# The end of the last batch in a two-layer graph kernel: a new order for GpSimd's work, for the norms of two older batches and for the last four rows

## The chip, the cores and the metric

The kernel runs on one NeuronCore of one Trainium2 chip. The metric is the device time of one execution in microseconds; 2596.31 us is the median of three runs of the kernel before (2594.66 to 2597.35). Five engines work from queues of their own: TensorE (PE in the profile, its weight loads PEld), VectorE (DVE), ScalarE (ACT), GpSimd (POOL) and SyncE (SP), which here issues nearly all the DMAs. An engine takes its instructions in the order in which the program lists them for that engine, and waits on semaphores of the others.

## The reference

32 batches of 512 rows by 512 features pass through two layers that share one 512x512 adjacency matrix of zeros and ones:

```
q, k, v = x@Wq+bq, x@Wk+bk, x@Wv+bv           # 8 heads of 64
s = softmax(q@k.T / 8, masked where adj == 0)
x = layernorm(x + s@v)                        # layer 0
x = layernorm(x + (adj@x)@weight + bias)      # layer 1
```

The layer norms go along the features, without gain or offset.

## The kernel before

**Tiling.** A batch is four blocks of 128 rows (`NB`) and four blocks of 128 features (`DB`). A 128x512 float32 result fills one PSUM bank; there are eight, all from one pool (`bank`, line 200). `X[b]` holds the rows of batch b in SBUF. The residuals, the norms and the output all happen in place in it.

**Products in halves.** Operands are split into a rounded high half and a rest, so that three passes of fast matmuls give float32 accuracy. For the second layer, `aggregate` (line 510) multiplies by the adjacency and yields, for each block d of features, one bank. `split_y` (line 504) turns that bank into three factors: the high one on ScalarE (line 303), the rest on VectorE (line 306), and their difference "both" on GpSimd or VectorE (line 309). `convolve` (line 555) then multiplies the factors by the weight: for each block r of rows, four matmuls each of HIGH and REST into a "near" bank and four of BOTH into a "far" bank. `add_row` (line 564) adds near (line 547) and far (line 551) to `X[b]` on VectorE. `add_bias` (line 530) adds the bias to a row block on GpSimd. `survey` lists `statistics` (lines 467 and 468, VectorE); `norm` lists a square root on ScalarE (line 471), its inverse with four shifts on VectorE (lines 476 and 478), and four `normalise` on ScalarE (line 483). `store` issues the output DMA from SP.

**The order of the work** is written out by hand: the pools run under a manual schedule, and the Python order of the calls is the order of each engine's queue. `run` executes a list of units, and `merge` lays other units behind them one by one. `iteration(b)` overlaps the attention of batch b, the projections of b+1 and the second layer of b-1. The first 31 batches go through it, and the change doesn't touch it, except that the norms and the store of the batch numbered 29 are left to what follows.

**The end**, which the change is about, consists of `last_halves(31)` and of the program's last part (line 928 on). Batches are numbered 0 to 31, so three of them are open here: 29 (rows 2 and 3 of its second layer, its second norm, its store), 30 (its whole second layer) and 31 (half of its attention and all that follows).

- `last_halves` ends the attention of 31. In between, it runs the last two row blocks of `convolve(29)`, adds their rows and biases, splits `X[30]` by feature blocks (`split`, line 486: the high on ScalarE, line 493, and the low on VectorE, line 494), folds the sums of the exponentials (`folds`, lines 645 and 647), sends them through memory and back to another layout (`pass_parts` and `fetch_parts`, lines 654 and 661), aggregates batch 30 (line 516), and then norms and stores batch 29 and adds the last attention results to `X[31]` (`add_up`, lines 667 to 669, and `last_residual`, lines 695 and 697).
- The program's last part takes statistics of `X[31]`, convolves batch 30, and then for each row block c: normalises `X[31]`'s block, adds batch 30's row c, splits `X[31]`'s block into a high (ScalarE, line 527) and a low (GpSimd, line 528), adds batch 30's bias (GpSimd, line 531) and takes its statistics. Then come the four biases of 31, `aggregate_rows(31)` (line 539: for each row block, four banks with one low and one high matmul each), its `split_y`, `convolve(31)` (48 matmuls), batch 30's norm and store, and row by row batch 31's near and far sums, statistics, root, inverse, normalise and store. `judge` (lines 701 to 706) and one small matmul (line 964) form a verdict (line 965) on whether the fast path's numbers can be trusted. A slower general kernel stands behind a branch on it and isn't executed here.

Of the kernel before, what the change touches and what calls it, by code (L numbers as in the profile page):

```python
# [182 lines left out]
def fast_kernel(ctx: ExitStack, tc, verdict, x, adj, Wq, bq, Wk, bk, Wv, bv, W1, b1, out):  # L183
    nc = tc.nc
    B, N, D = x.shape
    H = Wq.shape[1] // HD
    HP = H // 2
    NB = N // P
    DB = D // P
# [10 lines left out]
    def bank(*shape):  # L200

        return psum.tile([P, *shape], FP, name="bank", tag="bank", bufs=8)

    def plain(t):

        return t.bitcast(FP)
# [95 lines left out]
    def split_high(high, a):  # L302
        nc.scalar.activation(high, a, AF.Copy, scale=EPSILON * SHRINK)

    def split_rest(rest, high, a):
        nc.vector.scalar_tensor_tensor(rest, plain(high), -1.0 / EPSILON, a, op0=ALU.mult, op1=ALU.add)  # L306
# [18 lines left out]
    def factors():  # L325
        return [work.tile([P, DB, N], FR, name=f"factors{f}", bufs=1) for f in (HIGH, REST, BOTH)]
# [143 lines left out]
    def square_root(t, slots):  # L470
        nc.scalar.activation(RSTD[t][:, slots], STAT[t][:, slots, 1], AF.Sqrt, bias=eps)

    def invert_root(t, slots):

        rstd = RSTD[t][:, slots]
        nc.vector.reciprocal(rstd, rstd)
        for slot in range(slots.start, slots.stop):
            nc.vector.tensor_scalar(SHIFT[t][:, slot:slot + 1], STAT[t][:, slot, 0:1], RSTD[t][:, slot:slot + 1], -1.0,  # L478
                                    op0=ALU.mult, op1=ALU.mult)
# [6 lines left out]
    def split(b, d):  # L486

        cols = X[b][:, :, d * P:(d + 1) * P]
        room = d // PAIRS if b == B - 2 else 0
        high = work.tile([P, NB, P], FR, name="high", tag=f"q{room}", bufs=PAIRS)  # L490
        low = work.tile([P, NB, P], FR, name="low", tag=f"k{room}", bufs=PAIRS)
        HIGHS[b, d], LOWS[b, d] = high, low
        nc.scalar.activation(high, cols, AF.Copy)  # L493
        (nc.vector if b == B - 2 else nc.gpsimd).tensor_sub(low, cols, plain(high))  # L494

    def store(b, blocks=None):
        for c in blocks or ():
            nc.sync.dma_start(out[b, c * P:(c + 1) * P, :], X[b][:, c, :])
        if blocks is None:
            nc.sync.dma_start(out[b].rearrange("(c p) d -> p c d", p=P), X[b])  # L500

    YT = {}

    def split_y(b, d, pm, engine=nc.gpsimd):
        high, rest, both = (YT[b][f][:, d, :] for f in range(3))
        split_high(high, pm)
        split_rest(rest, high, pm)
        split_both(both, high, rest, engine)
# [24 lines left out]
    def aggregate_rows(b):  # L533

        banks = [bank(N) for _ in range(DB)]
        for c in range(NB):
            for d, pm in enumerate(banks):
                for part in (LOWS[b, c], HIGHS[b, c]):
                    nc.tensor.matmul(pm, part[:, d * P:(d + 1) * P], adjT[:, c, :],
                                     start=(c == 0 and part is LOWS[b, c]), stop=(c == NB - 1 and part is HIGHS[b, c]))  # L540
        YT[b] = factors()
        for d, pm in enumerate(banks):
            split_y(b, d, pm, nc.gpsimd if d < 2 else nc.vector)

    def add_near(b, r, near):
        row = X[b][:, r, :]
# [2 lines left out]
    def add_far(b, r, far):  # L549
        row = X[b][:, r, :]  # L550
        nc.vector.tensor_add(row, far, row)  # L551

    NEAR, FAR = {}, {}

    def convolve(b, passes):

        yt = YT[b]
        for r, f, blocks in passes:
            if (b, r) not in NEAR:
                NEAR[b, r], FAR[b, r] = bank(N), bank(N)  # L560
            one_pass(f, (FAR if f == BOTH else NEAR)[b, r], lambda f, d: yt[f][:, d, r * P:(r + 1) * P],
                     lambda f, d: w1[:, f, d, :], blocks)

    def add_row(b, r):
        add_near(b, r, NEAR.pop((b, r)))
        add_far(b, r, FAR.pop((b, r)))

    def whole(r):
        return [(r, f, range(DB)) for f in (HIGH, REST, BOTH)]
# [129 lines left out]
    def judge():  # L699
        seen = consts.tile([P, 3], FP, name="seen")  # L700
        nc.vector.tensor_reduce(seen[:, 0:2], watched.rearrange("p k c h -> p k (c h)"), axis=AX.X, op=ALU.add)
        nc.vector.tensor_reduce(seen[:, 2:3], inexact, axis=AX.X, op=ALU.add)
        well = consts.tile([P, 4], FP, name="well")
        nc.vector.tensor_scalar(well[:, 0:2], seen[:, 0:2], BOUND, None, op0=ALU.is_le)
        nc.vector.tensor_scalar(well[:, 2:3], seen[:, 2:3], 0.0, None, op0=ALU.is_equal)
        nc.vector.tensor_reduce(well[:, 3:4], well[:, 0:3], axis=AX.X, op=ALU.min)
        return well[:, 3:4]

    def run(units):
        for unit in units:  # L710
            unit[0](*unit[1:])
# [42 lines left out]
    def norm(t, which):  # L754

        if t - which < 0:
            return []
        lo, hi = which * NB, (which + 1) * NB
        return [(square_root, t, slice(lo, hi)), (invert_root, t, slice(lo, hi))] + [
            (normalise, t, slot) for slot in range(lo, hi)]  # L760
# [4 lines left out]
    def survey(b, which=1):  # L765

        return [(statistics, b, which, c) for c in range(NB)] if b >= 0 else []
# [5 lines left out]
    def biases(b):  # L773
        return [(add_bias, b, c) for c in range(NB)] if b >= 0 else []

    def merge(units, behind):

        merged = []
        for k in range(max(len(units), len(behind))):
            merged += units[k:k + 1] + (behind[k] if k < len(behind) else [])  # L780
        return merged
# [78 lines left out]
    def last_halves(b):  # L860

        splits, gathered = aggregation(b - 1)
        young = norm(b - 1, 0)
        attend(b, 0)
        turn_out(b, 0)
        attend(b, 1)
        turn_out(b, 1)
        fetch_parts(b, 0)
        add_up(b, 0)
        take_scores(b, 1)  # L870
        turn_back(b, 0)
        turn_back(b, 1)
        run(young[:1] + [(last_residual, b, 0), (last_residual, b, 1)] + young[1:2] + folds(b, 1)[:1])
        for r in range(NB // 2, NB):
            convolve(b - 2, whole(r))
        run([(add_row, b - 2, r) for r in range(NB // 2, NB)] + biases(b - 2)[NB // 2:] + young[2:] + splits)
        attend(b, 2)
        turn_out(b, 2)
        attend(b, 3)
        turn_out(b, 3)  # L880
        turn_back(b, 2)
        turn_back(b, 3)
        run(folds(b, 1)[1:] + [(pass_parts, b, 1), (fetch_parts, b, 1)])
        run(merge(gathered, [[unit] for unit in survey(b - 2)[NB // 2:]]) + norm(b - 1, 1))
        store(b - 2)
        run([(add_up, b, 1), (last_residual, b, 2), (last_residual, b, 3)])

    units = projections(0)
    ends = project_first_two()
# [36 lines left out]
    last_halves(B - 1)  # L926

    t = B - 1
    ahead, seen, next_ = norm(t, 0), survey(t - 1), norm(t, 1)
    run(survey(t, 0) + ahead[:2])  # L930
    convolve(t - 1, FIRST_TWO + whole(2) + whole(3))
    for c in range(NB):
        run(ahead[2 + c:3 + c] + [(add_row, t - 1, c)])
        split_rows(t, c)
        run(biases(t - 1)[c:c + 1] + seen[c:c + 1])
    run(biases(t))
    aggregate_rows(t)
    convolve(t, FIRST_TWO)
    run([(add_near, t, r, NEAR.pop((t, r))) for r in range(2)])
    run(next_)  # L940
    store(t - 1)
    well = judge()
    for table, name, shape in ((STAT, "stat", (2 * NB, 2)), (RSTD, "rstd", (2 * NB,)), (SHIFT, "shift", (2 * NB,))):
        table[t + 1] = work.tile([P, *shape], FP, name=name, bufs=3)
    for r in range(NB):
        if r < 2:
            add_far(t, r, FAR.pop((t, r)))
        else:
            convolve(t, whole(r))
            add_row(t, r)  # L950
        statistics(t, 1, r)
        slot = slice(NB + r, NB + r + 1)
        square_root(t + 1, slot)
        invert_root(t + 1, slot)
        if r == NB - 1:
            row = X[t][:, r, :]
            nc.vector.tensor_scalar(row, row, STAT[t + 1][:, NB + r, 0:1], RSTD[t + 1][:, NB + r:NB + r + 1],
                                    op0=ALU.subtract, op1=ALU.mult)
        else:
            normalise(t + 1, NB + r)  # L960
        store(t, [r])
        if r == 1:
            pm = bank(N)
            nc.tensor.matmul(pm[0:1, 0:1], well, ones[:, 0:1], start=True, stop=True)
            nc.vector.tensor_scalar(verdict, pm[0:1, 0:1], P - 0.5, None, op0=ALU.is_lt)


# [22 lines left out]
```

## Time and profile before

| | us |
|---|---|
| median of three runs | 2596.31 |
| the profiled execution, its own time | 2597.58 |
| its span in the trace | 2595.2 |
| TensorE busy | 2570.6 (99%) |
| VectorE busy | 2071.4 (80%) |
| ScalarE busy | 1527.2 (59%) |
| GpSimd busy | 1747.4 (67%) |
| last matmul of `convolve(30)` ends | about 2550.95 |
| first matmul of `aggregate_rows(31)` | 2552.46 |
| first matmul of `convolve(31)` | 2564.42 |
| last matmul ends | about 2584.3 |
| last VectorE instruction (line 957) ends | about 2590.5 |

Times are in microseconds from the start of the span. A line of the timeline gives the start, the duration (of the whole group, where equal instructions are merged), the engine, the line of the source, the operation with output and input, the number of instructions, and in brackets the idle time of that engine just before and what released it. In a table of windows, each engine has its busy time in the stretch and, in brackets, its number of instructions; PEclk is the TensorE clock granted, with 1.00 for full speed.

### The profile page before, as it was taken

To read this page: it belongs to the slowest core of one execution; us is meant where nothing else is said; L and a number is where in the kernel's file an instruction comes from. 1 tells how busy PE (TensorE), PEld (TensorE's weight loads), DVE (VectorE), ACT (ScalarE), POOL (GpSimd) and SP (SyncE) were. 2 spreads that over 40 slices of the span, in tenths; PEclk is the share of its full clock that TensorE was granted. 3 is DMA by queue.
4 is the path that set the end of the run, shared out by engine and by line. 5 is a ranking of instruction groups with operands and counts; after the bars stand their busy time and mean duration, and the time that the engine had idled before them with its cause. 6 is when DMAs were issued, how large, how long until landed. Compare 5 with 4: busy or idle time off the path is not lost.

```text
span 2595.2 us, 35714 instructions
## 1 busy us (share of the span) xinstructions
PE 2570.6 (99%) x11326; PEld 1696.3 (65%) x11326; DVE 2071.4 (80%) x3801; ACT 1527.2 (59%) x2539; POOL 1747.4 (67%) x1099
## 2 busy tenths in 40 slices
PE   9999999999999999999999999999999999999997
PEld 6666666766666666767666666667666666766665
DVE  8878888788787788877877878878778878788776
ACT  5566655656555666556565566655566655656553
POOL 4776676666676666767666766667666676666674
PEclk9999999999999999999999999999999999999998
DMA  8555554554545645446545455454464454554511
GB/s 256 164 165 140 161 148 120 171 144 157 166 100 161 176 130 158 130 134 172 141 159 148 112 164 162 145 161 117 144 176 137 154 142 124 167 146 155 165 41 51
DMA packets 674898, 380.47 MB, mean 147 GB/s; under 512 B 586896, under 2 KB 590992, under 8 KB 674704
## 3 DMA queue, kind: packets, MB, share of 16 engines
q1 hardware_dynamic: 674416, 377.61, 51.2%
q8 instruction: 92, 1.51, 0.2%
q14 instruction: 102, 0.84, 0.1%
q10 hardware_dynamic: 288, 0.52, 0.1%
HBM read 303.57 MB, written 74.45 MB: 146 GB/s over the span
## 4 chain that ended last, share of the span: by engine, by line
PE 96%; DVE 1%; SPq 1%; POOL 1%; ACT 0%; DMA 0%; issue 0%; DVEq 0%; POOLq 0%; ACTq 0%
PE bank L408 52%; PE bank L592 17%; PE bank L615 17%; PE bank L516 9%; SPq L232 0%; DVE bnst L467 0%; POOL xlast L531 0%; POOL xs L531 0%; SPq L635 0%; DMA stream<-kept_k 0%; SPq L240 0%; DMA xin<-in_x_dram 0%; DVE wv L314 0%; SPq L661 0%; POOL factors L309 0%
## 5 line engine op out<-in xcount | busy, mean ns | idle before, releaser
L596 ACT ACTIVATE e<-e 128x1024 f32<-128x1024 f32 x512 | 526.0, 1055 | 308.1 <-DVE e L594 269.2
L408 PE MATMUL bank<-factors,stream 128*128 128x512 f32 x3012 | 704.3, 393 | 1.0 <-ACT stream L313 0.7
L408 PEld LDWEIGHTS bank<-factors,stream 128*128 128x128 f32 x3012 | 560.2, 188 | 165.7 <-DVE e L594 23.5
L607 POOL TENSOR_TENSOR es<-es,e 128x1024 f32<-128x1024 f32 x256 | 616.0, 2406 | 20.1
L594 DVE SCALAR_TENSOR_TENSOR e<-gap,bank 128x512 f32<-128x512 uint8 x1024 | 617.6, 677 | 12.2 <-PE bank L592 12.2
L607 POOL TENSOR_TENSOR es<-e 128x1024 f32<-128x1024 f32 x128 | 305.9, 2390 | 426.4 <-ACT e L596 426.4
L592 PE MATMUL bank<-q,k 64*128 64x512 f32 x2048 | 465.0, 599 | 0.7 <-DVE e L594 0.7
L615 PE MATMUL bank<-e,v 128*64 128x512 f32 x2048 | 453.6, 595 | 0.0
L592 PEld LDWEIGHTS bank<-q,k 64*128 64x128 f32 x2048 | 204.2, 186 | 260.0 <-issue 158.0
L408 PE MATMUL bank<-w,factors 128*128 128x512 f32 x1536 | 358.3, 392 | 3.7 <-POOL factors L309 1.9
L408 PE MATMUL bank<-wv,factors 128*128 128x512 f32 x1536 | 353.5, 389 | 0.0
L309 POOL TENSOR_TENSOR factors<-factors,factors 128x512 fp32r<-128x512 f32 x253 | 322.6, 1295 | 34.4 <-DVE factors L306 30.3
L681 ACT ACTIVATE rows<-rows,zero,inverse 128x64 f32<-128x64 f32 x992 | 335.1, 430 | 6.9 <-DVE inverse L668 6.9
L408 PEld LDWEIGHTS bank<-w,factors 128*128 128x128 f32 x1536 | 289.4, 189 | 66.3 <-DVE factors L306 3.1
L408 PEld LDWEIGHTS bank<-wv,factors 128*128 128x128 f32 x1536 | 288.2, 188 | 60.6 <-DVE e L594 0.8
L615 PEld LDWEIGHTS bank<-e,v 128*64 128x64 f32 x2048 | 141.4, 137 | 278.4 <-issue 263.9
L493 ACT ACTIVATE high<-xs 128x512 fp32r<-128x512 f32 x124 | 74.4, 627 | 333.3 <-PE bank L516 333.2
L494 POOL TENSOR_TENSOR low<-xs,high 128x512 fp32r<-128x512 f32 x120 | 154.2, 1297 | 156.1 <-PE bank L516 156.1
L531 POOL TENSOR_TENSOR xs<-xs,b_r 128x512 f32<-128x512 f32 x124 | 160.2, 1292 | 129.1 <-DVE xs L551 129.1
L627 DVE STREAM_TRANSPOSE attT<-bank 128x512 f32<-128x512 f32 x124 | 87.5, 707 | 156.3 <-PE bank L615 156.3
L483 ACT ACTIVATE xs<-xs,shift,rstd 128x512 f32<-128x512 f32 x248 | 181.6, 805 | 27.3 <-DVE shift L478 27.3
L685 POOL TENSOR_TENSOR xs<-xs,rows 128x512 f32<-128x512 f32 x124 | 160.6, 1306 | 22.6 <-ACT rows L681 14.2
(98 smaller groups left out, 2449.3 us busy)
## 6 DMA issues: line engine op xcount, KB each, us to landing
stream<-kept_q SPq DMA_DIRECT2D x124, 768.0 KB, 5.7
stream<-kept_k SPq DMA_DIRECT2D x124, 768.0 KB, 4.4
xin<-in_x_dram SPq DMA_DIRECT2D x496, 64.0 KB, 2.3
turned<-attT SPq DMA_DIRECT2D x124, 256.0 KB, 3.0
rows<-turned SPq DMA_DIRECT2D x496, 64.0 KB, 2.5
xs<-in_x_dram SPq DMA_DIRECT2D x31, 1024.0 KB, 6.4
out_dram<-xs SPq DMA_DIRECT2D x31, 1024.0 KB, 5.2
part<-passed SPq DMA_DIRECT2D x256, 8.0 KB, 1.7
```

What stands on the lines that cost most here:

```text
L309: engine.tensor_sub(both, plain(high), plain(rest))
L408: nc.tensor.matmul(pm, left(f, d), right(f, d), start=(f != REST and d == 0), stop=(f != HIGH and d == DB - 1))
L483: nc.scalar.activation(row, row, AF.Identity, bias=SHIFT[t][:, slot:slot + 1], scale=RSTD[t][:, slot:slot + 1])
L516: nc.tensor.matmul(pm, part, adjT[:, n % NB, :], start=(n == 0), stop=(n == 2 * NB - 1))
L531: nc.gpsimd.tensor_add(X[b][:, c, :], X[b][:, c, :], b1_r)
L592: nc.tensor.matmul(ps[s], keys[:, j * P:(j + 1) * P], queries, start=True, stop=True)
L594: nc.vector.scalar_tensor_tensor(e[:, s, :], gap[:, j, :], NEG * root, ps[s], op0=ALU.mult, op1=ALU.add)
L596: nc.scalar.activation(e, e, AF.Exp, scale=1.0 / root)
L607: nc.gpsimd.tensor_add(ES[b, hp], ES[b, hp] if j > 1 else E[b, hp, 0], E[b, hp, j])
L615: nc.tensor.matmul(po[s * HD:(s + 1) * HD, :], V[b, j][:, h * HD:(h + 1) * HD], e[:, s, :], start=(j == 0), stop=(j == NB - 1))
L681: nc.scalar.activation(part, part, AF.Identity, bias=zero, scale=inverse[:, c, s:s + 1])
L685: nc.gpsimd.tensor_add(cols, cols, ROWS.pop((b, hp)))
```

## The change

In `last_halves(31)`, `X[30]`'s low halves go from VectorE to GpSimd. The biases of batch 29's rows 2 and 3, their statistics, the second norm of batch 29 and its store leave this function. The biases of batch 30 enter it. `add_up` and both `last_residual` are put between the third and the fourth `aggregate(30, d)`.

In the last part, `convolve(30)` is listed ahead of the statistics of `X[31]`. The loop over row blocks holds only the normalise and the split of `X[31]`. After it follow the four added rows of batch 30 and their statistics, batch 29's two biases, batch 31's four biases, batch 29's two statistics, the roots and inverses for batches 29 and 30, the four `normalise` of batch 29, its store, and `judge`. `aggregate_rows(31)` takes high before low, and its splits are listed as four pairs of high and rest, and then four "both". All of `convolve(31)` is listed at once, then the `normalise` and the store of batch 30. In the row loop, the near part of row r+1 is added between row r's root and its inverse. The verdict is read in the third row's turn.

```diff
-        (nc.vector if b == B - 2 else nc.gpsimd).tensor_sub(low, cols, plain(high))
+        nc.gpsimd.tensor_sub(low, cols, plain(high))
...
-                for part in (LOWS[b, c], HIGHS[b, c]):
+                for part in (HIGHS[b, c], LOWS[b, c]):
...
+        high, rest, both = ([YT[b][f][:, d, :] for d in range(DB)] for f in range(3))
         for d, pm in enumerate(banks):
-            split_y(b, d, pm, nc.gpsimd if d < 2 else nc.vector)
+            split_high(high[d], pm)
+            split_rest(rest[d], high[d], pm)
+        for d in range(DB):
+            split_both(both[d], high[d], rest[d], nc.gpsimd if d < 2 else nc.vector)
...
-        run([(add_row, b - 2, r) for r in range(NB // 2, NB)] + biases(b - 2)[NB // 2:] + young[2:] + splits)
+        run([(add_row, b - 2, r) for r in range(NB // 2, NB)] + young[2:] + splits)
...
-        run(merge(gathered, [[unit] for unit in survey(b - 2)[NB // 2:]]) + norm(b - 1, 1))
-        store(b - 2)
-        run([(add_up, b, 1), (last_residual, b, 2), (last_residual, b, 3)])
+        shift = biases(b - 1)
+        ends = [(last_residual, b, 2), (last_residual, b, 3)]
+        run(merge(gathered, [shift[:1], [], [(add_up, b, 1)] + ends, shift[1:]]))
...
-    ahead, seen, next_ = norm(t, 0), survey(t - 1), norm(t, 1)
+    ahead = norm(t, 0)
+    convolve(t - 1, FIRST_TWO + whole(2) + whole(3))
     run(survey(t, 0) + ahead[:2])
-    convolve(t - 1, FIRST_TWO + whole(2) + whole(3))
     for c in range(NB):
-        run(ahead[2 + c:3 + c] + [(add_row, t - 1, c)])
+        run(ahead[2 + c:3 + c])
         split_rows(t, c)
-        run(biases(t - 1)[c:c + 1] + seen[c:c + 1])
-    run(biases(t))
+    run([(add_row, t - 1, r) for r in range(NB)] + survey(t - 1))
+    run(biases(t - 2)[NB // 2:] + biases(t) + survey(t - 2)[NB // 2:] + norm(t - 1, 1)[:2] + norm(t, 1)[:2])
+    run(norm(t - 1, 1)[2:])
+    store(t - 2)
+    well = judge()
     aggregate_rows(t)
-    convolve(t, FIRST_TWO)
-    run([(add_near, t, r, NEAR.pop((t, r))) for r in range(2)])
-    run(next_)
+    convolve(t, FIRST_TWO + whole(2) + whole(3))
+    run(norm(t, 1)[2:])
     store(t - 1)
-    well = judge()
+    pm = bank(N)
+    nc.tensor.matmul(pm[0:1, 0:1], well, ones[:, 0:1], start=True, stop=True)
...
+    add_near(t, 0, NEAR.pop((t, 0)))
     for r in range(NB):
-        if r < 2:
-            add_far(t, r, FAR.pop((t, r)))
-        else:
-            convolve(t, whole(r))
-            add_row(t, r)
+        slot = slice(NB + r, NB + r + 1)
+        add_far(t, r, FAR.pop((t, r)))
         statistics(t, 1, r)
-        slot = slice(NB + r, NB + r + 1)
         square_root(t + 1, slot)
+        if r < NB - 1:
+            add_near(t, r + 1, NEAR.pop((t, r + 1)))
         invert_root(t + 1, slot)
...
-        if r == 1:
-            pm = bank(N)
-            nc.tensor.matmul(pm[0:1, 0:1], well, ones[:, 0:1], start=True, stop=True)
+        if r == NB - 2:
             nc.vector.tensor_scalar(verdict, pm[0:1, 0:1], P - 0.5, None, op0=ALU.is_lt)
```

More of the change, by code (lines that the diff above doesn't have):

```diff
@@ L537, in aggregate_rows @@
             for d, pm in enumerate(banks):
-                for part in (LOWS[b, c], HIGHS[b, c]):
+                for part in (HIGHS[b, c], LOWS[b, c]):
                     nc.tensor.matmul(pm, part[:, d * P:(d + 1) * P], adjT[:, c, :],
-                                     start=(c == 0 and part is LOWS[b, c]), stop=(c == NB - 1 and part is HIGHS[b, c]))
+                                     start=(c == 0 and part is HIGHS[b, c]), stop=(c == NB - 1 and part is LOWS[b, c]))
         YT[b] = factors()
+        high, rest, both = ([YT[b][f][:, d, :] for d in range(DB)] for f in range(3))
         for d, pm in enumerate(banks):
-            split_y(b, d, pm, nc.gpsimd if d < 2 else nc.vector)
+            split_high(high[d], pm)
+            split_rest(rest[d], high[d], pm)
+        for d in range(DB):
+            split_both(both[d], high[d], rest[d], nc.gpsimd if d < 2 else nc.vector)
     def add_near(b, r, near):
```

## The prediction

> **What bounds the kernel now.** I read the page first, then the chain of waits over its last 100 us, then the windows over the end, then each engine's timeline there.
>
> ```profile
> span 2595.2 us, 35714 instructions
> PE 2570.6 (99%) x11326; PEld 1696.3 (65%) x11326; DVE 2071.4 (80%) x3801; ACT 1527.2 (59%) x2539; POOL 1747.4 (67%) x1099
> ```
>
> TensorE bounds the whole, so an edit elsewhere pays only where TensorE waits. The windows say where (the columns are stretch, its length, busy time of PE, PEld, DVE, ACT, POOL, then clock, DMA share, GB/s):
>
> ```profile
> 2540.00:2550.00 10.00, 10.00 (x46) 8.18 (x45) 8.97 (x27) 4.45 (x8) 3.23 (x4) 1.00 0.30 108
> 2550.00:2560.00 10.00, 6.93 (x20) 4.81 (x19) 5.47 (x10) 5.03 (x8) 6.55 (x6) 0.71 0.00 0
> 2560.00:2570.00 10.00, 8.16 (x30) 5.46 (x28) 7.35 (x12) 2.36 (x5) 8.85 (x7) 0.95 0.01 2
> 2570.00:2580.00 10.00, 7.71 (x22) 5.05 (x21) 4.54 (x16) 2.41 (x4) 2.95 (x3) 0.66 0.00 0
> 2580.00:2596.00 16.00, 4.32 (x19) 3.22 (x18) 7.92 (x21) 4.03 (x8) 0.00 (x0) 0.76 0.36 135
> ```
>
> Until 2550 TensorE is full; then it idles, and its clock falls below 1.00. At full speed 48 matmuls take 11.07 us (line 408 from 2539.88), 0.23 each. After 2550.95 there are 32 + 48 left: 18.3 us. They end at 2584.3, so 15.0 us of the 33.3 are waits and half clock. What is waited for, on TensorE, then on GpSimd:
>
> ```profile
> 2552.46 1.20 PE L539 MATMUL bank<-adjT,halves 128*128 128x512 f32 x4 [1.51 <-POOL halves L528]
> 2555.22 9.37 PE L539 MATMUL bank<-adjT,halves 128*128 128x512 f32 x28 [1.56 <-DVE xs L547]
> 2564.42 3.50 PE L408 MATMUL bank<-w,factors 128*128 128x512 f32 x10
> 2569.57 0.74 PE L408 MATMUL bank<-w,factors 128*128 128x512 f32 x2 [1.65 <-DVE factors L306]
> ```
>
> ```profile
> 2560.94 1.28 POOL L528 TENSOR_TENSOR halves<-xlast,halves 128x512 fp32r<-128x512 f32 x1
> 2563.38 1.28 POOL L531 TENSOR_TENSOR xs<-xs,b_r 128x512 f32<-128x512 f32 x1 [1.15 <-DVE xs L551]
> 2564.62 5.44 POOL L531 TENSOR_TENSOR xlast<-xlast,b_r 128x512 f32<-128x512 f32 x4
> 2570.01 2.94 POOL L309 TENSOR_TENSOR factors<-factors,factors 128x512 fp32r<-128x512 f32 x2
> ```
>
> Each low half stands behind a bias that waits for VectorE's row, so the last low ends at 2562.2; and the two "both" stand behind five biases, until 2572.95. After TensorE's end VectorE sets the pace, one row in 3.4 us:
>
> ```profile
> 2583.45 0.67 DVE L547 SCALAR_TENSOR_TENSOR xlast<-bank,xlast 128x512 f32<-128x512 f32 x1
> 2584.22 0.69 DVE L551 TENSOR_TENSOR xlast<-bank,xlast 128x512 f32<-128x512 f32 x1
> 2584.95 0.69 DVE L467 BATCH_NORM_STATS2 bnst<-xlast 128x6 f32<-128x512 f32 x1
> 2585.68 0.18 DVE L468 BATCH_NORM_AGGREGATE stat<-bnst 128x2 f32<-128x6 f32 x1
> 2586.22 0.17 DVE L476 RECIPROCAL rstd<-rstd 128x1 f32<-128x1 f32 x1 [0.36 <-ACT rstd L471]
> 2586.42 0.21 DVE L478 TENSOR_SCALAR shift<-stat,rstd 128x1 f32<-128x1 f32 x1
> ```
>
> **What the Trainium skill says.** "TensorE: Matmul & The Clock Gate", Part 1: the array runs at half clock after about one idle window of 3.4 us, and is released by a busy one; the windows run freely. The trace agrees: the clock is 0.50 from about 2554.3 to 2561.1 and from 2571.3 to 2578.2, both times 6.8 us, and matmuls then take 0.43 us. The specification table of the same page has ScalarE, VectorE and GpSimd as strict first-in first-out queues; step 5 rests on it. "GPSIMD Engine Reference", section 1: its SBUF interfaces are shared with VectorE, contended by instructions with two SBUF inputs. The trace agrees: line 494 on VectorE beside line 531 took 1.2 us, while line 551, with one input in PSUM, takes 0.69; line 531 went from 1.28 to 1.48. "ScalarE: Activation LUTs", Table sets: identity and copy are in every set, so moved roots need no reload; the trace's end has one load at 2522.58, and the roots from 2540 to 2589 have none.
>
> **The change, step by step**, on the clock of this trace.
>
> 1. *Lows of batch 30 to GpSimd.* VectorE loses four of line 494, 4.67 us. GpSimd, free at 2530.08, loses two biases (2.96) and gains 4 x 1.28: lows ready at 2531.4, 2532.6, 2533.9, 2535.2. TensorE asks for them at 2533.52, 2535.34, 2537.16, 2538.97. Cost nothing; the cover is 2.1 us or more.
>
> 2. *The last fold.* It stood behind line 494 and took 2534.66 to 2537.12. It now runs 2530.1 to 2532.6. Its way through memory (one issue at 2537.15, four from 2538.61 to 2540.35, landing 1.7 us later) took 4.6 us, so the sums are there at 2537.2.
>
> 3. *Sums and residuals ahead of the fourth split.* VectorE does the third rest (line 306) from 2538.9 to 2539.55, the sums 0.6, the residuals 2.75 (2542.66 to 2545.41 before): 2542.9. Only then comes the fourth rest, 2540.71 before, now done at 2543.55; GpSimd's fourth "both" is done at 2544.85 (one bias in front of the second "both" pushes nothing: third "both" 2541.2). TensorE needs that rest after ten matmuls, at 2542.2: a stall of 1.3 us, and 0.15 for the "both". `convolve(30)` ends at 2552.4, not 2550.95. What hides it: VectorE, which gets to its last far sum only at 2552.9 (step 5). Without that cover it costs 1.45.
>
> 4. *`X[31]`'s norm and split.* Four statistics take 3.3 us: 2543.55 to 2546.85, where they ended at 2548.74. The first normalise starts at 2547.65 instead of 2549.57. ScalarE needs 1.37 per block for normalise and high. GpSimd has done batch 30's biases by 2548.7 (three from 2544.85) and makes lows without anything in between: 2550.4, 2551.8, 2553.1, 2554.5. So the aggregation runs without a gap from 2552.4 and ends at 2559.7 (32 x 0.227), against 2564.6. Gain 4.9.
>
> 5. *Norms of older rows ahead of the splits.* VectorE, after the inverses (2547.9): four added rows at 1.40 (2527.28 to 2528.68), 2553.5; four statistics, 2556.85; two of batch 29, 2558.5, whose biases GpSimd has made by 2557.05. Root 0.3, inverse with shifts: ScalarE's first `normalise` of batch 29 starts at 2559.3, and four take 2.95: 2562.25. Behind them in ScalarE's queue stand the four highs that TensorE waits for. The first could start at 2558.3, but ends at 2562.85; before it ended at 2563.9. So 3.9 of the 4.9 are given back, and TensorE idles for 3.2 us. The same pieces' removal from 2537 to 2545 gives nothing but step 3's room. SP's store of batch 29 waits to 2562.25; behind it stand only batch 30's (about 2567.3) and the row stores (from 2572): nothing late.
>
> 6. *Splits and `convolve(31)`.* Highs 2562.85, 2563.4, 2563.9, 2564.35; rests 2563.6 to 2565.4; judge (0.8) lies before them. GpSimd is through with its six biases at 2562.1, so its "both" end at 2565.0 and 2566.5; VectorE's two, contended (1.52 and 1.05 before), at 2566.8 and 2567.65. At full clock TensorE follows these and ends at 2575.1. But it has just idled for a window: at half clock from 2562.9, work up to the seventh matmul ends at 2566.1. If the clock returns there, TensorE ends at 2575.4; if it returns after two windows, as both times before, at 2577 to 2578. I take 2576.4. Before: 2584.3.
>
> 7. *Tail.* A row now costs far to statistics 0.73, statistics 0.73, aggregate 0.10, the next near 0.61 in place of the 0.36 wait for the root, inverse 0.20, shift 0.13: 2.50 against 3.4. Row 0's far sum can start at 2568.2 to 2569.9, so VectorE reaches row 3's at 2575.7 to 2577.4; TensorE's end plus the verdict's matmul and reading (0.35) gives 2576.75. From the last far sum to the last instruction is 2.87 (2587.64 to 2590.51), then 4.69 to the span's end with the last store.
>
> Sum: 2576.4 + 0.35 + 2.87 + 4.69 = 2584.3 against 2595.2, **10.9 us less**. The profiled execution's own time is 2597.58 (2.4 around the span), 1.27 above the median; 2596.31 - 10.9 = 2585.4. What a measurement can tell from no change is about 0.2%, 5.2 us.
>
> Unknown costs: the clock's phase, 2575.1 to 2578 at TensorE's end (-1.3 to +1.6); GpSimd's ops under contention, 1.28 to 1.5, six of them in front of batch 29's statistics (0 to +1.3); the next near could also hide fully behind the root (-0.25 per row).
>
> **Rivals.**
> - *The clock stays at half* until the end: 48 x 0.43 from 2562.9 with 0.4 of waiting end at 2583.9; plus 7.9, span 2591.8, time 2592.9: no change. For: the gap of 3.2 us, and ragged matmuls behind it. Against: twice the clock came back after 6.8 us behind similar gaps. One more window (10.2 us) instead ends TensorE at 2578.8: 2587.8.
> - *ScalarE's queue holds longer*: each microsecond by which batch 29's biases or statistics are late goes to the highs, one to one, and lengthens the half clock. Contention (1.3) plus a full two windows (1.6): 2588.3. More than 5.7 us late would be no change.
> - *The sums come late* (slower): step 3 makes VectorE wait at 2539.55 for a trip through memory, in front of the fourth rest, and so of `convolve(30)` and all else. The margin is 2.3 us; beyond it each microsecond counts whole. Over 13.2 us late, a trip of 17.8 instead of 4.6, it is slower than before; over 18.4 it shows: 2602. Against: the four fetches landed in 1.4 to 1.8 us, on queues as empty then as now.
>
> **How the numbers follow.** The forecast with its bounds (2582.5 to 2588) has 0.62; a longer hold or one more cold window, 2588 to 2591, has 0.22; no change, by the clock or by a hold of over 5.7 us, 0.11; slower, 0.05. Faster is 0.62 + 0.22 = 0.84. The range is 2582.5 to 2590.5.
>
> **What would show it.** Lows on GpSimd from 2530; a TensorE gap of about 1.3 us near 2542; line 539 in one piece of 7.3 us; TensorE idle about 3 us after it, with ScalarE in line 483 for batch 29; clock 0.50 after that; VectorE rows 2.5 us apart. Wrong if line 539 still waits for lows, if the highs start as soon as line 539's banks close, or if TensorE's last matmul ends past 2581.

## The result, and the profile after

| | before | changed |
|---|---|---|
| median, us (six runs each) | 2596.53 | 2582.64 |
| all runs, us | 2594.66 to 2597.39 | 2582.31 to 2585.13 |
| profiled execution, its own time | 2597.58 | 2585.13 |
| its span | 2595.2 | 2582.9 |

The ratio is 0.9952, with a 95% interval from 0.9942 to 0.9962: faster by 12.5 us, between 10 and 15. The medians differ by 13.9; two later sets gave 11.1 each (the rows "changed, again" and "changed, a third time" of the table below). The forecast was 10.9 us less, 2585.4; the measured 2582.64 lies just above its lower bound of 2582.5.

The page's head, and the windows over the end (columns as before):

```profile
span 2582.9 us, 35712 instructions
PE 2565.6 (99%) x11326; PEld 1697.3 (66%) x11326; DVE 2066.9 (80%) x3797; ACT 1527.0 (59%) x2539; POOL 1751.5 (68%) x1103
```

```profile
2540.00:2550.00 10.00, 8.75 (x38) 6.67 (x37) 9.18 (x22) 3.49 (x6) 7.14 (x8) 1.00 0.00 1
2550.00:2560.00 10.00, 9.10 (x41) 7.20 (x39) 9.15 (x30) 4.56 (x9) 9.74 (x9) 1.00 0.01 2
2560.00:2570.00 10.00, 8.33 (x29) 6.46 (x30) 7.86 (x17) 6.17 (x11) 3.80 (x4) 0.83 0.55 210
2570.00:2584.00 14.00, 4.80 (x23) 3.64 (x21) 7.08 (x20) 3.33 (x6) 0.00 (x0) 0.83 0.22 80
```

As many matmuls as before, and the same busy share over the whole: 99% hides it. The stretch from 2550 to 2560 holds 41 matmuls at full clock, where it held 20 at 0.71. VectorE and GpSimd are over 9 of 10 us busy in it; they fill the time in which they waited for each other. In the first stretch TensorE has a hole that it didn't have.

The timelines of TensorE, GpSimd and ScalarE over the same end, lines numbered in the changed kernel (from 540 up to the program's last part they lie four higher):

```profile
2542.71 9.14 PE L408 MATMUL bank<-w,factors 128*128 128x512 f32 x38 [1.25 <-DVE factors L306]
2551.69 7.42 PE L539 MATMUL bank<-adjT,halves 128*128 128x512 f32 x32
2561.67 13.02 PE L408 MATMUL bank<-w,factors 128*128 128x512 f32 x48 [2.56 <-ACT factors L303]
2574.61 0.19 PE L949 MATMUL bank<-ones,well 128*1 128x1 f32 x2
```

```profile
2548.31 5.52 POOL L528 TENSOR_TENSOR halves<-xlast,halves 128x512 fp32r<-128x512 f32 x4 [0.55 <-ACT halves L527]
2553.78 2.54 POOL L531 TENSOR_TENSOR xs<-xs,b_r 128x512 f32<-128x512 f32 x2
2556.28 4.99 POOL L531 TENSOR_TENSOR xlast<-xlast,b_r 128x512 f32<-128x512 f32 x4
2562.41 2.53 POOL L309 TENSOR_TENSOR factors<-factors,factors 128x512 fp32r<-128x512 f32 x2 [1.14 <-DVE factors L306]
```

```profile
2557.41 0.48 ACT L471 ACTIVATE rstd<-stat,eps 128x4 f32<-128x4 f32 x2 [4.95 <-DVE stat L468]
2558.20 2.93 ACT L483 ACTIVATE xs<-xs,shift,rstd 128x512 f32<-128x512 f32 x4 [0.31 <-DVE shift L478]
2561.04 2.02 ACT L303 ACTIVATE factors<-bank 128x512 fp32r<-128x512 f32 x4
```

The aggregation (line 539) is one piece of 7.4 us, where it was 12.1, with one wait in front of it, one inside it, and 6.8 us at half clock. The four lows run in one piece, and GpSimd's first "both" starts at 2562.41 instead of 2570.01. TensorE then waits 2.56 us for the highs, and those stand behind batch 29's four normalise, as step 5 said. A row on VectorE:

```profile
2572.38 0.68 DVE L555 TENSOR_TENSOR xlast<-bank,xlast 128x512 f32<-128x512 f32 x1
2573.10 0.69 DVE L467 BATCH_NORM_STATS2 bnst<-xlast 128x6 f32<-128x512 f32 x1
2573.83 0.18 DVE L468 BATCH_NORM_AGGREGATE stat<-bnst 128x2 f32<-128x6 f32 x1
2573.93 0.67 DVE L551 SCALAR_TENSOR_TENSOR xlast<-bank,xlast 128x512 f32<-128x512 f32 x1
2574.52 0.15 DVE L476 RECIPROCAL rstd<-rstd 128x1 f32<-128x1 f32 x1
2574.71 0.21 DVE L478 TENSOR_SCALAR shift<-stat,rstd 128x1 f32<-128x1 f32 x1
```

The near part of the next row starts 0.10 behind the aggregate and covers the root; there is no wait left in the row, which takes 2.45 us. (The last row, with no near part behind it, still waits 0.36 us for its root.)

### The profile page after: what moved, and what is told of

It reads as the page before. It is cut to its first block, busy times and chain, and to the rows that moved or that the text cites. A ratio compares the mean times of both kernels' runs of the same rounds, so it can differ in the third digit from the quotient of the medians.

```text
span 2582.9 us, 35712 instructions
## 1 busy us (share of the span) xinstructions
PE 2565.6 (99%) x11326; PEld 1697.3 (66%) x11326; DVE 2066.9 (80%) x3797; ACT 1527.0 (59%) x2539; POOL 1751.5 (68%) x1103
## 3 DMA queue, kind: packets, MB, share of 16 engines
q1 hardware_dynamic: 674416, 377.61, 51.2%
## 4 chain that ended last, share of the span: by engine, by line
PE 97%; DVE 1%; SPq 1%; DMA 0%; ACT 0%; issue 0%; DVEq 0%
PE bank L408 53%; PE bank L596 18%; PE bank L619 17%; PE bank L516 9%; SPq L232 0%; DVE bnst L467 0%; SPq L240 0%; SPq L639 0%; DMA stream<-kept_k 0%; SPq L665 0%; DMA xin<-in_x_dram 0%; DVE xlast L555 0%; ACT xs L483 0%; DVE stat L468 0%; DVE xlast L551 0%
## 5 line engine op out<-in xcount | busy, mean ns | idle before, releaser
L598 DVE SCALAR_TENSOR_TENSOR e<-gap,bank 128x512 f32<-128x512 uint8 x1024 | 617.9, 681 | 11.8 <-PE bank L596 11.8
```

The source lines that it names most:

```text
L598: nc.vector.scalar_tensor_tensor(e[:, s, :], gap[:, j, :], NEG * root, ps[s], op0=ALU.mult, op1=ALU.add)
```

## The experiments

**How they are compared.** Up to the aggregation of batch 30 (line 516) TensorE's work is the same, but the profiles reach its first matmul between 2531.66 and 2533.41: 1.75 us that have nothing to do with the edits. So an edit of a microsecond or two isn't read from the median alone. I take two lengths from each profile, from that first matmul's start: to the end of the last VectorE instruction, and to the span's end (the last store adds 4.7 to 5.2). The three profiles of the changed kernel differ by 0.4 in the first length and by 0.5 in the second; every other kernel has one profile.

| kernel | median, us | before beside it | ratio, 95% interval | to last VectorE | to span's end |
|---|---|---|---|---|---|
| before | 2596.53 | | | 58.0 | 62.7 |
| changed | 2582.64 | 2596.53 | 0.9952 (0.9942 to 0.9962) | 46.1 | 51.2 |
| older norm behind the highs | 2583.78 | 2597.10 | 0.9948 (0.9935 to 0.9962) | 44.3 | 49.4 |
| lows on VectorE | 2584.62 | 2597.10 | 0.9952 (0.9939 to 0.9966) | 45.9 | 50.7 |
| sums last | 2588.01 | 2597.10 | 0.9967 (0.9955 to 0.9979) | 47.7 | 52.7 |
| row loop alone, on before | 2592.32 | 2597.10 | 0.9982 (0.9975 to 0.9989) | 53.3 | 58.2 |
| changed, again | 2585.06 | 2596.19 | 0.9953 (0.9940 to 0.9967) | 46.4 | 51.1 |
| all behind the splits | 2584.73 | 2596.19 | 0.9952 (0.9938 to 0.9965) | 45.1 | 50.3 |
| gap filled with matmuls | 2584.23 | 2596.19 | 0.9952 (0.9938 to 0.9965) | 45.5 | 50.6 |
| biases between the lows | 2593.62 | 2596.19 | 0.9989 (0.9983 to 0.9996) | 54.4 | 59.4 |
| what the runs point to | 2581.46 | 2596.40 | 0.9940 (0.9926 to 0.9954) | 43.5 | 48.5 |
| changed, a third time | 2585.26 | 2596.40 | 0.9951 (0.9937 to 0.9966) | 46.0 | 50.7 |

My theory was the prediction's: a chain of queues from VectorE over ScalarE and GpSimd to TensorE, with GpSimd's order as its largest piece. The rivals: the gain is TensorE's clock; or it is the rows' pace at the end.

**Biases between the lows again.** Batch 30's biases, added rows and statistics go back into the loop, so that GpSimd's and VectorE's order there changes together:

```diff
-        shift = biases(b - 1)
...
-        run(merge(gathered, [shift[:1], [], [(add_up, b, 1)] + ends, shift[1:]]))
+        run(merge(gathered, [[], [], [(add_up, b, 1)] + ends]))
...
-        run(ahead[2 + c:3 + c])
+        run(ahead[2 + c:3 + c] + [(add_row, t - 1, c)])
         split_rows(t, c)
-    run([(add_row, t - 1, r) for r in range(NB)] + survey(t - 1))
+        run(biases(t - 1)[c:c + 1] + survey(t - 1)[c:c + 1])
```

> The changed kernel, with batch 30's biases, added rows and statistics back in the loop of batch 31's normalise and split, in the order of before: GpSimd has each bias, which waits for VectorE's added row, between two lows. Theory (GpSimd's order is the main part of the change): the last low is done 12.65 us behind the first normalise instead of 7.1, line 539 stalls and ends about 2.6 us later; the biases of 29 and 31 come behind that, up to 10.2 us later than now, batch 29's statistics wait for them, and ScalarE's highs wait for these: about 7.9 us later. From the aggregation's first matmul to the end 59.1, up to 60.9 with a longer half clock; median about 2591. Rival (only the lows matter, later waits are hidden): +2.6, 53.8. Rival (the row loop is the main part): +1 or less.

Measured: 59.4 to the span's end, near the theory's 59.1. The median is 8.6 us above the changed kernel's on the same chip, and 2.6 above the 2591 that was expected. TensorE's lines, then GpSimd's and ScalarE's:

```profile
2552.99 6.22 PE L539 MATMUL bank<-adjT,halves 128*128 128x512 f32 x25
2560.76 1.88 PE L539 MATMUL bank<-adjT,halves 128*128 128x512 f32 x7 [1.54 <-POOL halves L528]
2570.82 13.44 PE L408 MATMUL bank<-w,factors 128*128 128x512 f32 x48 [8.19 <-ACT factors L303]
```

```profile
2561.87 3.72 POOL L531 TENSOR_TENSOR xs<-xs,b_r 128x512 f32<-128x512 f32 x3 [1.17 <-DVE xs L555]
2566.57 0.48 ACT L471 ACTIVATE rstd<-stat,eps 128x4 f32<-128x4 f32 x2 [12.84 <-DVE stat L468]
```

The lows cost TensorE 1.54 us. The larger part, 8.19 us, comes later: the three biases at 2561.87 are batch 30's last and batch 29's two; batch 29's statistics wait for these, and its root, its normalise and then ScalarE's highs wait for the statistics. To the last VectorE instruction it is 54.4, 8.2 us more than the changed kernel's mean, where before and the changed kernel are 11.8 apart. So the order in this loop is the largest piece tried. All the rest of the change without it is even 1.1 us longer than the row loop alone (53.3, next experiment), so the rows' pace isn't the main gain, though it is a large one. The two pieces, 8.2 and 4.7, sum to more than the whole: each was measured in other company, and they aren't shares of 11.8. Of TensorE's clock, this run shows that it is a small part of the 8.2: `convolve(31)` takes 13.44 us here and 12.90 to 13.29 in the changed kernel. What the clock cost in the kernel before was not tried by itself; 2.6 us of work were lost to it in the last 11.3 us, as the next experiment shows.

**The row loop alone**, put into the kernel before:

```diff
-    convolve(t, FIRST_TWO)
-    run([(add_near, t, r, NEAR.pop((t, r))) for r in range(2)])
+    convolve(t, FIRST_TWO + whole(2) + whole(3))
     run(next_)
     store(t - 1)
     well = judge()
```

with the verdict's matmul and the row loop of the change behind it.

> The kernel before (median 2596.53), with only the row loop of the change: all of convolve(31) listed at once, the near parts amid the roots, the verdict read in the third turn. My theory: TensorE ends where it did (about 2584.3), row 0's far sum comes at 2573.6 instead of 2578.31, and the last rows follow TensorE: the last far sum at 2584.6 instead of 2587.64, so 3.0 us less than before, 2593.5. Rival (the rows' pace on VectorE is the main gain): most of the 13.9 us, 2586 or less.

Measured: 4.75 us less in the profile, 4.8 in the medians. The expectation held VectorE's part but took TensorE's end as fixed. The last 35 matmuls took 1.7 us less. In before, they are the lines at 2573.01 and 2578.57 of its timeline, with the verdict's between them; here they are one line:

```profile
2573.01 5.06 PE L408 MATMUL bank<-w,factors 128*128 128x512 f32 x11 [0.43 <-POOL factors L309]
2578.45 0.19 PE L964 MATMUL bank<-ones,well 128*1 128x1 f32 x2 [0.38 <-DVE well L706]
2578.57 5.75 PE L408 MATMUL bank<-w,factors 128*128 128x512 f32 x24
```

```profile
2573.70 9.63 PE L408 MATMUL bank<-w,factors 128*128 128x512 f32 x35 [0.45 <-POOL factors L309]
2583.26 0.19 PE L943 MATMUL bank<-ones,well 128*1 128x1 f32 x2
```

Of the 1.7 us, 0.38 is the wait for the judging, which stood in the middle of TensorE's stream and now stands at its end. About 1.0 is clock: the mean granted over this stretch was 0.77 of 11.3 us before and 0.84 of 9.6 us here, which is 2.6 and 1.5 us of lost work. Where the half clock falls wasn't controlled, so that this second part belongs to the edit isn't shown.

**Older norm behind the highs** (the test of step 5):

```diff
-    run(norm(t - 1, 1)[2:])
-    store(t - 2)
     well = judge()
     aggregate_rows(t)
+    run(norm(t - 1, 1)[2:])
+    store(t - 2)
```

> The changed kernel (median 2582.64), with one edit: the normalise of batch 29 on ScalarE, and its store, come behind the four highs that TensorE waits for, not ahead of them. My theory (a chain of queues: VectorE's statistics and inverses, ScalarE's normalise, the highs): the highs start when the first bank of line 539 closes, about 2.9 us sooner, but VectorE's inverses and the judging still stand before the rests, so these come only 1.3 us sooner, and GpSimd's four biases hold its first difference (line 309) to 1.1 us sooner. The end comes 1.2 us sooner; TensorE idles under 0.5 us behind line 539, so its clock may also stay full, for another 0.8: 2580.6 to 2581.4. Rival (the idle gap in front of convolve(31) is what counts, with its half clock): the whole 2.6 us come back, and the clock with them: 2579 or less.

Measured: 44.3 against 46.0 to 46.4, so 1.7 to 2.1 less, at the upper edge of the theory. The highs come as soon as the banks close and the clock stays at 1.00 to the end, but VectorE goes on with inverses and judging until 2562.02, and isn't idle for a moment from there to the last row's root. TensorE's 2.56 us of waiting were worth less than they looked: VectorE was the next in line. The medians (13.3 us under before, with the change at 11.1 to 13.9) can't tell this edit from none.

**The gap filled**, to keep the clock up without moving anything:

```diff
     aggregate_rows(t)
+    filled = bank(N)
+    for _ in range(10):
+        nc.tensor.matmul(filled, adjT[:, 0, 0:P], adjT[:, 0, :], start=True, stop=True)
     convolve(t, FIRST_TWO + whole(2) + whole(3))
```

> The changed kernel, with ten matmuls of no use (128x128 by 128x512, into a bank that nobody reads) behind line 539, which fill TensorE's 2.56 us of waiting for the highs with about 2.3 us. Theory (the half clock behind that wait is the smaller part of it; the rests and boths set the pace of convolve(31)'s first half): the clock stays at 1.00, row 0's far part is done about 0.9 us sooner, and so is the end: 50.3 us from the aggregation's first matmul to the end against 51.2. Rival (the clock is what the gap costs): a stretch of 3.4 us at half clock is 1.7 us of matmuls, so 49.5. Rival (the gap alone, not the clock): no change.

Measured: 45.5 to the last VectorE instruction, or 0.5 to 0.9 less than the changed kernel's three profiles; to the span's end it is 50.6, only 0.1 to 0.6 less. That speaks against the rival of 1.7 us. Between the theory's 0.9 and no change at all, this one profile decides only weakly.

```profile
2560.53 2.43 PE L947 MATMUL bank<-adjT 128*128 128x512 f32 x10
2563.25 12.29 PE L408 MATMUL bank<-w,factors 128*128 128x512 f32 x48 [0.30 <-ACT factors L303]
```

`convolve(31)` takes 12.29 us instead of 13.02 at a clock of 1.00, and still not 11.07: the rests and the differences set its first half. The 3.4 us of half clock (0.87 on the mean of the changed kernel's 13 us, 1.7 us of work) are at least half hidden.

**Lows on VectorE** (the test of steps 1 and 2): the one line of `split` as before.

```diff
-        nc.gpsimd.tensor_sub(low, cols, plain(high))
+        (nc.vector if b == B - 2 else nc.gpsimd).tensor_sub(low, cols, plain(high))
```

> The changed kernel, with the four lows of batch 30 back on VectorE. My theory: they take 4.7 us ahead of the last fold, so the sums land 4.6 us later, at about 2541.0 on the changed kernel's clock, while VectorE asks for them at 2538.65. It waits 2.35 us in front of the fourth rest; TensorE's stall in convolve(30) grows from 1.25 to about 3.6 us, and all behind it moves by 2.3 us: 2585.0. Rival (this end of the fold is hidden, the gain comes from the later parts alone): no change, 2582.6.

A miss: 45.9, no change. The same four lows, before and here, each with what GpSimd ran next:

```profile
2530.07 4.67 DVE L494 TENSOR_TENSOR low<-xs,high 128x512 fp32r<-128x512 f32 x4
2530.03 2.96 POOL L531 TENSOR_TENSOR xs<-xs,b_r 128x512 f32<-128x512 f32 x2
```

```profile
2529.49 2.48 DVE L494 TENSOR_TENSOR low<-xs,high 128x512 fp32r<-128x512 f32 x4
2531.89 1.29 DVE L649 STREAM_TRANSPOSE square<-es 128x512 f32<-128x512 f32 x2
...
2538.30 0.69 DVE L306 SCALAR_TENSOR_TENSOR factors<-factors,bank 128x512 fp32r<-128x512 f32 x1 [1.13 <-ACT factors L303]
2538.98 0.27 DVE L671 TENSOR_REDUCE inverse<-part 128x16 f32<-128x64 f32 x1
2535.50 1.30 POOL L309 TENSOR_TENSOR factors<-factors,factors 128x512 fp32r<-128x512 f32 x1 [6.00 <-DVE factors L306]
```

With GpSimd's two biases gone from beside them, four lows take 2.48 us and not 4.67: before, the two that ran beside the biases took 1.79 and 1.76 us each, and the two behind them 0.68, as all four do here. The fold is 2.4 us later than in the changed kernel, not 4.6, and the sums (line 671) still find their data within 0.1 us of when VectorE asks. Moving the biases away had already brought what the move of the lows was to bring.

**Sums last** (the test of step 3's cover):

```diff
-        run(merge(gathered, [shift[:1], [], [(add_up, b, 1)] + ends, shift[1:]]))
+        run(merge(gathered, [shift[:1], [], [], shift[1:]]) + [(add_up, b, 1)] + ends)
```

> The changed kernel, with the sums and the residuals of batch 31 behind the fourth rest again. My theory: TensorE's stall of 1.25 us in convolve(30) goes, and that convolution ends 1.35 us sooner; but VectorE does the same work up to the statistics, which start at the same time, so the aggregation's splits come at the same time, TensorE idles longer in front of them, and the end doesn't move: 2582.6, within 0.5. Rival (the stall is on the path): 1.3 us sooner, 2581.3.

A miss too: 47.7, so 1.2 to 1.7 us more. TensorE's stall goes, and `convolve(30)` is one piece of 11.04 us; but VectorE then stands idle in front of the fourth rest:

```profile
2539.04 0.69 DVE L306 SCALAR_TENSOR_TENSOR factors<-factors,bank 128x512 fp32r<-128x512 f32 x1 [1.13 <-ACT factors L303]
2540.85 0.69 DVE L306 SCALAR_TENSOR_TENSOR factors<-factors,bank 128x512 fp32r<-128x512 f32 x1 [1.13 <-ACT factors L303]
2541.46 0.26 DVE L671 TENSOR_REDUCE inverse<-part 128x16 f32<-128x64 f32 x1
```

In the changed kernel the sums and residuals lie in that 1.13 us. All of VectorE's later work starts 1.3 us later here. The stall is not what holds the end up, as step 3 had it; what the expectation forgot is that the same instructions in another order leave an idle piece on the engine that is.

**All behind the splits**, to see whether emptying the queues ahead of the highs brings more than the norm alone:

```diff
-    run(biases(t - 2)[NB // 2:] + biases(t) + survey(t - 2)[NB // 2:] + norm(t - 1, 1)[:2] + norm(t, 1)[:2])
-    run(norm(t - 1, 1)[2:])
-    store(t - 2)
+    run(biases(t - 2)[NB // 2:] + survey(t - 2)[NB // 2:])
     well = judge()
     aggregate_rows(t)
+    run(biases(t) + norm(t - 1, 1)[:2] + norm(t, 1)[:2])
     convolve(t, FIRST_TWO + whole(2) + whole(3))
+    run(norm(t - 1, 1)[2:])
+    store(t - 2)
...
-            split_both(both[d], high[d], rest[d], nc.gpsimd if d < 2 else nc.vector)
+            split_both(both[d], high[d], rest[d], nc.vector if d == 2 else nc.gpsimd)
```

> The changed kernel, with four things moved behind the splits of aggregate_rows(31) or in front of them: batch 29's and 30's roots and inverses, batch 29's normalise and store and batch 31's biases go behind, the judging goes ahead of the aggregation's splits into VectorE's wait for the highs, and VectorE makes one 'both' (the third) instead of two. Theory (VectorE's queue is the bound from the statistics to the end, TensorE's half clock is a consequence): the first rest comes 1.9 us sooner than with ScalarE's norm alone moved (49.4 us from the aggregation's first matmul to the end), VectorE is then late only by the inverses (1.4), and the end comes 1.0 to 1.65 sooner: 47.8 to 48.4, which is 2.8 to 3.4 less than the change, a median near 2579.5. Rival (ScalarE's queue was the only thing): 49.4, as with that one edit alone.

A miss: 50.3 to the span's end (45.1), worse than with the norm alone. TensorE ended 39.5 us behind the aggregation's start, 1.6 sooner than there, and it didn't help, because VectorE met two new waits:

```profile
2566.14 0.69 DVE L551 SCALAR_TENSOR_TENSOR xlast<-bank,xlast 128x512 f32<-128x512 f32 x1 [1.02 <-POOL xlast L531]
...
2570.08 0.16 DVE L476 RECIPROCAL rstd<-rstd 128x1 f32<-128x1 f32 x1 [0.92 <-ACT rstd L471]
```

Row 0's bias now stood behind GpSimd's three differences, and row 0's root behind eight normalise of older batches on ScalarE. Both are pieces that "cost nothing" where the change has them.

**What the runs point to.** Only the pieces that VectorE's queue asks for: judging in the wait for the roots, inverses ahead of the rests, two biases of batch 31 ahead and two behind, one "both" on VectorE, normalise of batch 29 behind the highs.

```diff
-            split_both(both[d], high[d], rest[d], nc.gpsimd if d < 2 else nc.vector)
+            split_both(both[d], high[d], rest[d], nc.vector if d == 2 else nc.gpsimd)
...
-    run(biases(t - 2)[NB // 2:] + biases(t) + survey(t - 2)[NB // 2:] + norm(t - 1, 1)[:2] + norm(t, 1)[:2])
-    run(norm(t - 1, 1)[2:])
+    older, old = norm(t - 1, 1), norm(t, 1)
+    run(biases(t - 2)[NB // 2:] + biases(t)[:2] + survey(t - 2)[NB // 2:] + older[:1] + old[:1])
+    well = judge()
+    run(older[1:2] + old[1:2])
+    aggregate_rows(t)
+    run(biases(t)[2:])
+    convolve(t, FIRST_TWO + whole(2) + whole(3))
+    run(older[2:])
     store(t - 2)
-    well = judge()
-    aggregate_rows(t)
-    convolve(t, FIRST_TWO + whole(2) + whole(3))
-    run(norm(t, 1)[2:])
+    run(old[2:])
     store(t - 1)
```

> The changed kernel with what the runs so far point to. Of batch 29's norm only the roots stand ahead of the highs; its normalise and store come behind. The judging comes ahead of the inverses, into VectorE's wait for the roots. VectorE makes one 'both' instead of two. Only two of batch 31's four biases stand ahead of GpSimd's differences, so that row 0's bias is done when VectorE asks for it. Theory (from the statistics on, VectorE's queue sets the end; a piece taken off it or put into a wait of it counts whole): rests begin 27.5 us behind the aggregation's first matmul (28.6 with ScalarE's norm alone moved), the far sum of row 0 at 32.5 (34.0), and the last VectorE instruction ends at 42.8 to 43.2, against 46.1 and 46.4 in the two profiles of the change, 44.3 with the norm alone and 45.1 with all behind. Median 3 us under the change on the same chip. Rival (ScalarE's eight normalise ahead of the rows' roots, or GpSimd's late differences, take the place of what is removed, as in the run before): 44.3 or more, and no gain over the norm alone.

The changed kernel was run once more in each of the last two sets:

> The changed kernel once more, unedited, so that the edits of this set are compared with it on one chip, and so that a second profile shows how far the clock and the steady part differ between executions. The profile of the change needs 51.2 us from the first matmul of batch 30's aggregation to the span's end (62.7 before); I expect 51.2 within 0.9, by the clock's phase, and a median 12 to 14.5 us under the kernel before.

> The changed kernel a third time, unedited, as the measure for the other run on this chip. 46.1 to 46.9 us from the first matmul of batch 30's aggregation to the last VectorE instruction's end; a median 11 to 14 us under the kernel before.

Of these two repeats, both medians came out 11.1 us under the kernel before, where the first had 12 to 14.5 expected; the second's profile, with 46.0, is 0.1 under its range.

Measured for what the runs point to: 43.5 to the last VectorE instruction, against 46.0 for the change on that chip (the shortest of its three profiles). The miss of 0.3 at least is in the far sum of row 0, which waits for TensorE:

```profile
2565.51 7.78 PE L408 MATMUL bank<-w,factors 128*128 128x512 f32 x33 [0.64 <-POOL factors L309]
2566.05 0.69 DVE L555 TENSOR_TENSOR xlast<-bank,xlast 128x512 f32<-128x512 f32 x1 [1.13 <-PE bank L408]
```

It came at 33.1, not 32.5, because GpSimd's three differences took 4.24 us beside VectorE's own, 1.4 each instead of 1.28. Here VectorE waits for TensorE again, and TensorE for GpSimd. The medians, 2581.46 and 2585.26, differ by 3.8 us, but single runs overlap (2580.46 to 2583.29, 2581.68 to 2585.91): the gain over the change, 2.5 us in one profile and 3.8 in the medians of five runs each, is likely and not beyond doubt. It is clearly faster than the kernel before.

## Why the prediction was right

The waits that it named came where it named them, and the sum by stages comes close. Its 10.9 us are 1.5 by which `convolve(31)` starts sooner, 6.4 in it and 3.0 behind it; measured were 1.9, 6.9 and 3.1, together 11.9.

Times in us behind the first matmul of batch 30's aggregation (2532.50 before, 2531.66 in the changed kernel's profile):

| step | predicted | measured |
|---|---|---|
| 3: stall in `convolve(30)` for the fourth rest | 1.3 | 1.25 |
| 3: line 539 starts | 19.9 | 20.0 |
| 4: line 539 ends | 27.2 | 27.5 |
| 5: TensorE idle in front of `convolve(31)` | 3.2 | 2.56 |
| 5: first high done | 30.4 | 30.0 |
| 6: TensorE's last matmul of `convolve(31)` ends | 43.9 (42.6 to 45.5) | 43.0 |
| 7: one row | 2.50 | 2.45 |
| last VectorE instruction ends | 47.1 | 46.1, 46.4, 46.0 |

- *Steps 1 and 2* are right as facts: the lows run on GpSimd from 2529.19 in 5.00 us, in time, and the fold runs 4.5 us sooner. As causes they are empty: with lows on VectorE the end is the same.
- *Step 3* priced the stall to 0.05 us and named the right cover, but the cover is thinner than forecast: `convolve(30)` ends at 2551.85 and VectorE takes its last far sum at 2551.90, about 0.05 us later, where 0.5 had been expected. A clearly longer stall would probably have counted; that was not tried. It didn't say what the new order is worth, 1.2 to 1.7 us, although its own numbers contain it (statistics at 2543.55 instead of 2545.45).
- *Step 4* holds. Undoing it costs 8.2 us, most of it through step 5's chain.
- *Step 5* holds in its place and nearly in its size: 0.6 us less idle, half because line 539 ended 0.3 later and half because batch 29's normalise started 0.3 sooner than I had added up.
- *Step 6* took a half clock of more than one window; all three profiles of the change have one of 3.4 us. TensorE ended 0.9 us sooner than forecast, inside the bounds given: 0.4 of it because the highs came sooner (step 5), and 0.5 because `convolve(31)` took 13.0 us instead of 13.5. That is still 0.5 more than the prediction had for a single window, so the lucky phase of the clock is only part of this.
- *Step 7* holds, except that TensorE's end and the reading of the verdict didn't set the end: VectorE's rows follow one another without a wait from row 0's far sum (2567.47) to the last row's (2574.91), some 0.2 us behind the end of TensorE's last matmul of `convolve(31)`. On the kernel before, the row loop alone brought 4.7 us rather than the roughly 3 that its VectorE part amounts to.
- *The rivals.* The clock came back, after one window of 3.4 us. ScalarE's queue held as long as forecast and no longer. The trip through memory was in time: the fold ended at 2531.73, and VectorE took the sums at 2538.65 without a wait.
- *The remaining difference.* The span fell by 12.3 us in the profile: 11.9 between the two marks, 0.8 ahead of them, and minus 0.4 in the last store. The 0.8 is there ahead of the first edited instruction: GpSimd's sums of the exponentials (line 607, now 611) start at 2521.91 instead of 2522.76. That the medians differ by 13.9 once and by 11.1 twice may be of that kind, which the prediction doesn't contain. That the first set's median lies inside its bounds, by 0.1 us, is therefore partly luck; the medians of the later two sets lie within 0.4 of the forecast 2585.4. What moves the steady part by a microsecond or two between executions was not looked into.

## What to carry to other kernels

A short instruction in an in-order queue costs what the queue behind it costs: look up who waits for the next instruction, and the one after. Where several engines hand work in a circle, find the one whose idle pieces the end follows (here mostly VectorE), and judge each reordering by whether it fills or opens an idle piece there; a stall of TensorE beside it may be free, and a filled gap of TensorE may bring little. Price a moved operation with its neighbours as they will be: its duration before may have been the contention with something that moves away as well.

## What the runs showed of the hardware that was not expected

- Two of the four subtractions of line 494, which have two SBUF inputs, ran on VectorE while GpSimd added biases (2530.03 to 2532.99), and took 1.79 and 1.76 us. The other two took 0.68, as did all four in the run in which GpSimd was idle. "GPSIMD Engine Reference", section 1, names the shared interfaces; the runs add the price, about 1.1 us for each such instruction. The 1.2 us that the prediction read from line 494 lies between these two groups and holds for neither.
- The half clock between the aggregation of 31 and the last matmul comes in lengths of one unit of 3.4 us: one in the three profiles of the changed kernel and with the lows on VectorE (TensorE had waited 2.56 to 2.58 us), two with the sums last (4.67 us), three with the biases between the lows (8.19 us), none in the kernels in which TensorE's longest wait was 1.25 us. "TensorE: Matmul & The Clock Gate", Part 1, has the window of 3.4 us, and in length these runs agree with it. Its condition, about one idle window, they don't show: some 2.6 us of idling were enough in those four profiles, and in the kernel before two waits of 1.5 us with 1.2 us of work between them. There, two units followed; behind the same two waits in the run with the row loop alone, one. The prediction's "the trace agrees" holds for the length alone. In the run that filled the gap, the unit turned out to have cost 0.5 to 0.9 us to the last VectorE instruction, not the 1.7 us of matmul work in it.
